# Attention outputs of a graph layer: turned in 32x32 blocks by VectorE and exchanged by DMA, in place of four TensorE transposes

## The chip, the cores and the metric

The kernel runs on one core of a Trainium2 chip. The metric is the device time of one execution in microseconds, lower is better. Engines are named as in the profile: PE is TensorE (PEld its weight loads), DVE is VectorE, ACT is ScalarE, POOL is GpSimd, SP is SyncE, which computes nothing here but issues nearly all DMAs.

## The reference, cut to what matters

There are 16 graphs (B = 16) of N = 1024 nodes with D = 256 features, and a 0/1 adjacency matrix each. Two layers follow each other. The first is multi-head attention with a mask, then an MLP; the second a graph attention that isn't touched here. The part that matters:

```python
normed = layer_norm(x, gamma1, beta1)
qkv = normed.reshape(b_, n_, H, HD).transpose(0, 2, 1, 3)      # H = 8 heads, HD = 32
scores = einsum('bhqd,bhkd->bhqk', qkv, qkv) * scale
attn = softmax(where(adj > 0, scores, -inf))
out = einsum('bhqk,bhkd->bhqd', attn, qkv)
x = x + out.transpose(0, 2, 1, 3).reshape(b_, n_, d_)
y = layer_norm(x, gamma2, beta2)
x = x + gelu(y @ W1 + b1) @ W2 + b2
```

All data are fp32, except the mask, which is held in an 8-bit float.

## The kernel before, in words

`tile_gnn_kernel` calls `fast_path`, and after it a general path that runs only where a flag asks for it; it isn't run on these inputs. `fast_path` is unrolled over all 16 graphs.

**Attention** (`attention`, L966). A graph is done in 32 *units* (`units`, L1048), over two halves of 512 queries (`qh`), in each over two groups of four heads (`g`), in each over eight tiles of 128 keys (`kt`). `scores` (L971) makes the score matmuls (L987) for a unit with keys on partitions and queries along the free dimension, four heads into two PSUM tiles; DVE adds the mask (L1000) and ACT takes the exponential (L1007), whose accumulator gives the softmax denominators `den`, as the mask is symmetric. `weigh` (L1017) multiplies by the values (L1022) into one PSUM tile `o` of 128 x 512, with the 32 features of the four heads on partitions and 512 queries along the free dimension. The pool of `o` has one buffer. Its result has to be turned, since the residual `h` has queries on partitions.

**Turning it** (`finish`, L951). After the eighth tile of keys DVE copies `o` into `os` (L1031). Later PE transposes four 128 x 128 blocks of it into PSUM (`ptos`, L958), DVE multiplies by the reciprocal sums `rl` and writes `ot` (L960), and POOL adds that to `h` (L964). This happens four times a graph, 64 times in all. `invert` (L1038) makes the reciprocals (L1043, L1044), which are complete only in the second half of the queries.

**The rest of a graph** (`rest`, L1100, a generator; call it stream B, and attention stream A). Rows of `h` are taken in four chunks of 256. For a chunk `c`, `prepare` (L1078) measures the norm of `h` on DVE (L739, L740, L742), lets POOL take a power (L744), and normalizes on DVE (L748); `turn` (L1133) transposes on PE (`pty`, L1143), with the scaled result `yT` (L1147); `expand` is the first product (`ph`, L572, evacuated into `hid` by DVE, L1170), and `contract` the second (`po`, L572, added to `xb` by DVE, L1197). `add_residuals` has POOL add bias and residual (L1113, L1114). Then comes the second layer, whose PE work is `lg`, `pa`, `pf`, `pg`, `puT`, and `store` (L1318) with its store L1321. The last outputs of a graph are made by `tails[b]` within the next graph's `rest`.

**What sets the order.** Stream A of graph b + 1 and stream B of graph b are interleaved by a planner at build time (from L1411): each piece has a *place*, and a `clock` that adds up estimated PE time (2.0 per unit of A, the number yielded by each piece of B). `defer(us, f)` emits `f` when that clock has advanced by so much, `turns` holds transposes that PE makes between units, and `make_turns` (L938) emits them. The order thus planned is kept on every engine: the last lines of `fast_path` chain each engine's instructions in the order in which they were emitted. So each engine, SP among them, works through a fixed list and waits at the head of it. `finished` counts the outputs that have been added to `h`; chunks 0 and 1 need those of the first half of the queries (both groups), and chunks 2 and 3 those of the second.

**Masks.** `turn_masks` (L889) fetches adjacency tiles with two DMAs each (L585) into two buffers, converts them on DVE (L592), and a transposing DMA (L902) brings them to the layout that the scores need; `compare_masks` (L909) compares on POOL (L917), with an accumulation on DVE (L924), that the mask is symmetric. All DMAs share eight completion semaphores in turn, and a DMA is issued only when the one eight before it has landed.

Of the kernel before, what the change touches and what calls it, by code (L numbers as in the profile page):

```python
# [9 lines left out]
F32 = mybir.dt.float32  # L10
# [5 lines left out]
ALU = mybir.AluOpType  # L16

P = 128
# [477 lines left out]
def fast_path(  # L496
# [28 lines left out]
    nc = tc.nc  # L525
# [22 lines left out]
    hp = pool("hp", 2)  # L548
    vp = pool("vp", 2)
    midp = pool("midp", 3)  # L550
    ep = pool("ep", 6)
    denp = pool("denp", 2)
    lp1 = pool("lp1", 6)
    tmpp = pool("tmpp", 2)
    smallp = pool("smallp", 3)
# [4 lines left out]
    def ps_tile(shape, name, dtype=F32):  # L560
        return psm.tile(shape, dtype, tag="ps", name=name)
# [386 lines left out]

    finished = {}

    def finish(b, qh, g, rl, ready, os):  # L951
        h = hs[b]
        run_deferred(ready)
        finished[b, qh] = finished.get((b, qh), 0) + 1
        clock[0] += 0.5
        pt = ps_tile([P, TPH, P], f"ptos_{b}_{g}_{qh}")
        for t in range(TPH):
            nc.tensor.transpose(pt[:, t, :], os[:, t * P : (t + 1) * P], ident)  # L958
        ot = tmpp.tile([P, TPH, GH, HD], F32, tag="w2", bufs=5, name=f"ot_{b}_{g}_{qh}")
        nc.vector.tensor_mul(  # L960
            ot, pt.rearrange("p t (j d) -> p t j d", d=HD), rl.unsqueeze(3).to_broadcast([P, TPH, GH, HD])
        )
        ho = h[qh][:, :, g * P : (g + 1) * P]
        nc.gpsimd.tensor_add(ho, ho, ot.rearrange("p t j d -> p t (j d)"))  # L964

    def attention(b, st):  # L966
        va, kT = st["va"], st["kT"]
        den = denp.tile([P, NQH, NT, H], F32, tag="den", name=f"den_{b}")


        def scores(qh, g, kt):  # L971
            qs = slice(qh * QW, (qh + 1) * QW)
            sc = [
                psc.tile([P, 2, QW], F32, tag=f"sc{i}", name=f"s_{b}_{g}_{qh}_{kt}_{i}") for i in range(2)
            ]
# [18 lines left out]
            mb = st[qh][:, kt // 2, :, kt % 2].unsqueeze(1).to_broadcast([P, 2, QW])  # L994
            es = []
            for i in range(2):
                e = ep.tile([P, 2, QW], F32, tag="e", name=f"e_{b}_{g}_{qh}_{kt}_{i}")
                masked = sc[i]
                if 2 * i >= by_pe:
                    nc.vector.tensor_tensor(e, masked, mb, op=ALU.add)  # L1000
                    masked = e
                es.append(e)

                def weights(e=e, masked=masked, i=i):
                    for j in range(2):
                        n = g * GH + 2 * i + j
                        nc.scalar.activation(  # L1007
                            e[:, j], masked[:, j], AF.Exp, scale=SCALE, accum_out=den[:, qh, kt, n : n + 1]
                        )

                if i == 0:
                    weights()
            return es, weights

        acc, os, rl = {}, {}, {}

        def weigh(qh, g, kt, es):  # L1017
            if kt == 0:
                acc[g, qh] = pso.tile([P, QW], F32, tag="o", name=f"o_{b}_{g}_{qh}")
            o = acc[g, qh]  # L1020
            for j in range(GH):
                nc.tensor.matmul(  # L1022
                    o[j * HD : (j + 1) * HD, :],
                    va[:, kt, (g * GH + j) * HD : (g * GH + j + 1) * HD],
                    es[j // 2][:, j % 2, :],
                    start=(kt == 0),
                    stop=(kt == NT - 1),
                )
            if kt == NT - 1:
                c = os[g, qh] = tmpp.tile([P, QW], F32, tag="w2", bufs=5, name=f"os_{b}_{g}_{qh}")  # L1030
                nc.vector.tensor_copy(c, o)  # L1031
                if qh == NQH - 1:
                    close(qh, g)

        def close(qh, g):
            turns.append((1, lambda: finish(b, qh, g, *rl[g, qh], os[g, qh])))

        def invert(qh, g):  # L1038
            r = smallp.tile([P, TPH, GH], F32, tag="rl", name=f"rl_{b}_{g}_{qh}")
            ts, hs_ = slice(qh * TPH, (qh + 1) * TPH), slice(g * GH, (g + 1) * GH)  # L1040

            def f():
                nc.vector.tensor_tensor(r, den[:, 0, ts, hs_], den[:, 1, ts, hs_], op=ALU.add)  # L1043
                nc.vector.reciprocal(r, r)  # L1044

            rl[g, qh] = r, defer(2.5, f)

        units = [(qh, g, kt) for qh in range(NQH) for g in range(NG) for kt in range(NT)]  # L1048
        for u in units:
            make_turns()  # L1050
            es, rest_of_weights = scores(*u)
            go_on()
            rest_of_weights()
            scored.append((weigh, (*u, es)))
            qh, g, kt = u
            if qh == NQH - 1 and kt % TPH == TPH - 1:
                invert(kt // TPH, g)
                if kt < NT - 1:
                    close(kt // TPH, g)
            yield  # L1060

    def go_on():
# [37 lines left out]
    def rest(b, st, tails):  # L1100
# [230 lines left out]
        hid = {0: (yield from expand(0))}  # L1331
        ask(turn, 1)
        yield from tails[b]()
        while finished.get((b, 1), 0) < NG:
            yield 0.0, None
        prepare(b, st, 2)
        load(2)
        hid[1] = yield from expand(1)
        ask(turn, 2)
        prepare(b, st, 3)  # L1340
        yield from contract(0, hid[0])
# [84 lines left out]
    def stream_b():  # L1426
        for b in range(B):
            done = 0.0
            place = b + 0.99
            yield place  # L1430
            for us, others in states[b]["rest"]:
                clock[0] += us
                done += us
                if others is None:

                    if places[1] is None:
                        make_turns()
                    else:
                        place = max(place, places[1] + 1e-6)
                elif others:  # L1440
                    place = max(place, b + 1 + done / B_US)
                yield place
        for us, _ in tails[B]():
            clock[0] += us
            yield B + 1
# [115 lines left out]
```

## Time and profile before

| | |
|---|---|
| Time, median of 3 runs | 3426.13 us (3424.79 to 3426.3) |
| Profiled execution: its own time, its span | 3422.06 us, 3420.3 us |
| Granted TensorE clock | 0.999 |
| `ptos` transposes on PE (L958) | 256, 41.9 us busy |
| Copy `os` from PSUM on DVE (L1031) | 64, 681 ns each |
| Product `ot` on DVE (L960) | 64, 692 ns each |
| Sum into `h` on POOL (L964) | 64, 1284 ns each |
| SP, issue of one store of 128 KB (L1321) | 0.34 us, landed after 1.7 us |
| SP, issue of one mask fetch of 256 KB (L585) | 0.37 us, landed after 3.6 us |
| SP, issue of one transposing DMA (L902) | 1.2 us, landed after 3.9 us |

How to read it: times of single instructions come from one profiled execution; a matmul's end is modelled, so that matmuls that follow each other overlap by a few hundredths of a microsecond in the timeline. The share of an engine is its busy time over the span. A number in brackets behind an instruction is the time that its engine stood idle ahead of it, and what ended that.

### The profile page before, as it was taken

What the parts mean: (1) busy time and instruction counts of PE and PEld (TensorE: products, weight loads), DVE (VectorE), ACT (ScalarE), POOL (GpSimd) and SP (SyncE); (2) the same over time, 40 slices, a digit from 0 to 9 for tenths busy, and PEclk for the clock granted to TensorE, in tenths of its full rate; (3) what the DMA queues carried; (4) which work ended last, traced back from release to release, by engine and by line L of the source; (5) the groups of instructions that cost most, each with busy time, mean ns of one, the idle gap of its engine ahead of it and who ended that gap; (6) DMA issues with size and microseconds to landing.
All of it is one profiled execution on the core that took longest, in us unless ns stands there. A gap on an engine that the chain in (4) does not pass through costs nothing. (4 is left out here: it accounts for less than half of the span.)

```text
span 3420.3 us, 114618 instructions
## 1 busy us (share of the span) xinstructions
PE 3356.2 (98%) x49790; PEld 1603.4 (47%) x49790; DVE 2799.1 (82%) x5427; ACT 2061.6 (60%) x5192; POOL 880.6 (26%) x1038
## 2 busy tenths in 40 slices
PE   6899999999999999999999999999999999999998
PEld 1244444444444444444444444444444444444477
DVE  6788888888888978888888887888879788897854
ACT  6665666656566565666656656666665655666532
POOL 3422232222323222232222312223222232321120
PEclk9999999999999999999999999999999999999999
DMA  4111202112011121111211112120211211111000
GB/s 135 45 39 40 57 17 54 39 47 56 20 46 39 48 54 34 40 31 48 54 39 48 25 50 45 42 56 18 52 39 48 55 26 40 39 48 42 8 19 14
DMA packets 157471, 145.22 MB, mean 42 GB/s; under 512 B 81056, under 2 KB 116256, under 8 KB 156960
## 3 DMA queue, kind: packets, MB, share of 16 engines
q1 hardware_dynamic: 156672, 137.56, 15.8%
q8 instruction: 392, 6.42, 0.8%
q14 instruction: 119, 0.97, 0.1%
q10 hardware_dynamic: 288, 0.26, 0.0%
HBM read 104.21 MB, written 16.78 MB: 35 GB/s over the span
## 5 line engine op out<-in xcount | busy, mean ns | idle before, releaser
L1007 ACT ACTIVATE e<-e 128x512 f32<-128x512 f32 x1984 | 1224.8, 619 | 960.5 <-DVE e L1000 958.1
L1000 DVE TENSOR_TENSOR e<-s,mk 128x1024 f32<-128x1024 f32 x992 | 1168.1, 1218 | 195.2 <-PE s L987 192.7
L987 PE MATMUL s<-kT 32*64 32x512 f32 x8192 | 579.5, 615 | 1.1 <-DVE e L1000 0.9
L1022 PE MATMUL o<-e,va 128*32 128x512 f32 x4096 | 557.5, 606 | 1.3 <-ACT e L1007 1.3
L572 PE MATMUL lg<-fT,uT 128*32 128x256 f32 x7680 | 454.1, 379 | 0.0
L572 PE MATMUL pa<-gw,e 128*32 128x258 f32 x7552 | 453.3, 380 | 0.0
L572 PE MATMUL ph<-yT,w 128*32 128x256 f32 x7808 | 451.0, 379 | 0.0
L572 PE MATMUL po<-w,hid 128*32 128x256 f32 x7680 | 438.9, 379 | 0.0
L1007 ACT ACTIVATION_READ_ACCUMULATOR e<-e 128x1 f32 x1984 | 371.2, 187 | 0.0
L572 PEld LDWEIGHTS ph<-yT,w 128*32 128x32 f32 x7808 | 255.5, 110 | 213.0 <-issue 55.7
L572 PEld LDWEIGHTS lg<-fT,uT 128*32 128x32 f32 x7680 | 257.3, 110 | 200.5 <-issue 43.3
L572 PEld LDWEIGHTS pa<-gw,e 128*32 128x32 f32 x7552 | 252.3, 110 | 206.6 <-issue 56.5
L572 PEld LDWEIGHTS po<-w,hid 128*32 128x32 f32 x7680 | 249.6, 110 | 209.6 <-issue 62.8
L1022 PEld LDWEIGHTS o<-e,va 128*32 128x32 f32 x4096 | 83.6, 108 | 424.6 <-issue 198.9
L1267 DVE SCALAR_TENSOR_TENSOR e<-lg,gw,mk 128x256 f32<-128x256 f32 x512 | 221.7, 474 | 64.2 <-PE lg L572 37.4
L1273 ACT ACTIVATE e<-e,shift 128x512 f32<-128x512 f32 x256 | 182.2, 715 | 141.5 <-DVE e L1272 103.8
L964 POOL TENSOR_TENSOR h<-h,ot 128x512 f32<-128x512 f32 x64 | 84.7, 1323 | 697.8 <-DVE ot L960 697.8
L917 POOL TENSOR_TENSOR odd<-mk,mq 128x512 bf16<-128x512 fp8e5 x192 | 233.3, 1216 | 100.2 <-DVE uneven L924 100.2
L1170 DVE TENSOR_TENSOR hid<-ph,b1c 128x512 f32<-128x512 f32 x256 | 173.6, 683 | 77.8 <-PE ph L572 67.8
L1272 DVE SCALAR_TENSOR_TENSOR e<-e 128x512 f32<-128x512 f32 x256 | 209.5, 818 | 8.8
L987 PEld LDWEIGHTS s<-kT 32*64 32x64 f32 x8192 | 122.7, 130 | 161.0 <-issue 105.0
L744 POOL TENSOR_TENSOR rs_c<-ve_c,mhalf 128x2 f32<-128x2 f32 x64 | 44.5, 695 | 477.4 <-DVE ve_c L742 378.1
(135 smaller groups left out, 3477.0 us busy)
## 6 DMA issues: line engine op xcount, KB each, us to landing
adj<-in_adj_dram SPq DMA_DIRECT2D x248, 256.0 KB, 3.6
h<-in_x_dram SPq DMA_DIRECT2D x64, 256.0 KB, 4.0
xb<-in_x_dram SPq DMA_DIRECT2D x128, 128.0 KB, 2.3
out_dram<-z SPq DMA_DIRECT2D x128, 128.0 KB, 1.7
adj<-in_adj_dram SPq DMA_DIRECT2D x4, 512.0 KB, 7.0
mk<-mq SPq DMA_TRANSPOSE x128, 3.8
w<-in_L_gnn_W_dram SPq DMA_DIRECT2D x2, 1024.0 KB, 8.7
wo<-in_L_gnn_W_dram SPq DMA_DIRECT2D x2, 256.0 KB, 9.8
```

What stands on the lines that cost most here:

```text
L572: nc.tensor.matmul(out[c : c + HD], lhsT[:, c : c + HD], rhs, start=start, stop=stop)
L744: nc.gpsimd.tensor_tensor(rs, ve, mhalf[:, :nt], op=ALU.pow)
L917: nc.gpsimd.tensor_tensor(odd.rearrange("p (u v x) -> p u v x", u=2, v=2), key.rearrange("p (u v x) -> p u v x", u=2, v=2), query.rearrang ...
L964: nc.gpsimd.tensor_add(ho, ho, ot.rearrange("p t j d -> p t (j d)"))
L987: nc.tensor.matmul(sc[j // 2][c : c + P // 2, j % 2, :], kT[r, g, kt * P + c : kt * P + c + P // 2], kT[r, g, qs], start=j >= by_pe, stop= ...
L1000: nc.vector.tensor_tensor(e, masked, mb, op=ALU.add)
L1007: nc.scalar.activation(e[:, j], masked[:, j], AF.Exp, scale=SCALE, accum_out=den[:, qh, kt, n : n + 1])
L1022: nc.tensor.matmul(o[j * HD : (j + 1) * HD, :], va[:, kt, (g * GH + j) * HD : (g * GH + j + 1) * HD], es[j // 2][:, j % 2, :], start=(kt = ...
L1170: nc.vector.tensor_tensor(hid[:, f0 : f0 + 2, :], ph, b1c[:, f0 : f0 + 2].unsqueeze(2).to_broadcast([P, 2, CW]), op=ALU.add,)
L1267: nc.vector.scalar_tensor_tensor(e[:, j, :], lg[:, j, :], gw[:, kt, D : D + 1], st[c // 2][:, kt // 2, qs, kt % 2], op0=ALU.add, op1=ALU.add,)
L1272: nc.vector.scalar_tensor_tensor(e, e, ALPHA, e, op0=ALU.mult, op1=ALU.max)
L1273: ready = defer(2.5, lambda: nc.scalar.activation(e, e, AF.Exp, bias=shift))
```

## The change

DVE's copy of `o` becomes a transpose of 32x32 blocks straight from PSUM into a tile `x`, named `xo` in the profile. Within each block features and queries change places, but the blocks of the four heads are still on four groups of 32 partitions. Sixteen plain DMAs of 16 KB (32 partitions of 512 bytes) then move them, so that each head's block comes to the partitions of its queries: `move(j)` issues four of them, and is deferred by 2, 5, 8 and 11 us of the planner's clock. POOL multiplies by the reciprocal sums and adds to `h`. `finish` and its entry in `turns` are gone; `close` is deferred by 16 us (second half of the queries) or 4.5 us. In `rest`, the check of `finished` and `prepare(b, st, 2)` come after `expand(1)`. The pool `ep` has five buffers for six, the tag `w2` four for five, and a pool `turnp` with one buffer holds `x`. One `clock` addition moves into the planner's loop.

```diff
-    ep = pool("ep", 6)
+    ep = pool("ep", 5)
+    turnp = pool("turnp", 1)
...
-    def finish(b, qh, g, rl, ready, os):
-        h = hs[b]
-        run_deferred(ready)
-        finished[b, qh] = finished.get((b, qh), 0) + 1
-        clock[0] += 0.5
-        pt = ps_tile([P, TPH, P], f"ptos_{b}_{g}_{qh}")
-        for t in range(TPH):
-            nc.tensor.transpose(pt[:, t, :], os[:, t * P : (t + 1) * P], ident)
-        ot = tmpp.tile([P, TPH, GH, HD], F32, tag="w2", bufs=5, name=f"ot_{b}_{g}_{qh}")
-        nc.vector.tensor_mul(
-            ot, pt.rearrange("p t (j d) -> p t j d", d=HD), rl.unsqueeze(3).to_broadcast([P, TPH, GH, HD])
-        )
-        ho = h[qh][:, :, g * P : (g + 1) * P]
-        nc.gpsimd.tensor_add(ho, ho, ot.rearrange("p t j d -> p t (j d)"))
...
             if kt == NT - 1:
-                c = os[g, qh] = tmpp.tile([P, QW], F32, tag="w2", bufs=5, name=f"os_{b}_{g}_{qh}")
-                nc.vector.tensor_copy(c, o)
+                x = turnp.tile([P, GH, TPH, HD], F32, tag="block", name=f"xo_{b}_{g}_{qh}")
+                nc.vector.transpose(x, o.rearrange("p (t a i) -> p a t i", t=TPH, a=GH))
+                c = os[g, qh] = tmpp.tile([P, GH, TPH, HD], F32, tag="w2", bufs=4, name=f"os_{b}_{g}_{qh}")
+
+                def move(j):
+                    for a in range(GH):
+                        nc.sync.dma_start(c[a * HD : (a + 1) * HD, j], x[j * HD : (j + 1) * HD, a])
+
+                for j in range(GH):
+                    defer(2.0 + 3.0 * j, lambda j=j: move(j))
                 if qh == NQH - 1:
-                    close(qh, g)
-
-        def close(qh, g):
-            turns.append((1, lambda: finish(b, qh, g, *rl[g, qh], os[g, qh])))
+                    close(qh, g, 16.0)
+
+        def close(qh, g, us):
+            def f():
+                finished[b, qh] = finished.get((b, qh), 0) + 1
+                c = os[g, qh].rearrange("p j t d -> p t j d")
+                ho = hs[b][qh][:, :, g * P : (g + 1) * P].rearrange("p t (j d) -> p t j d", d=HD)
+                nc.gpsimd.tensor_mul(c, c, rl[g, qh].unsqueeze(3).to_broadcast([P, TPH, GH, HD]))
+                nc.gpsimd.tensor_add(ho, ho, c)
+
+            defer(us, f)
...
-                    close(kt // TPH, g)
+                    close(kt // TPH, g, 4.5)
...
         yield from tails[b]()
+        hid[1] = yield from expand(1)
         while finished.get((b, 1), 0) < NG:
             yield 0.0, None
         prepare(b, st, 2)
         load(2)
-        hid[1] = yield from expand(1)
         ask(turn, 2)
...
                         make_turns()
+                        clock[0] += 0.5
```

More of the change, by code (lines that the diff above doesn't have):

```diff
@@ L1029, in weigh @@
             if kt == NT - 1:
-                c = os[g, qh] = tmpp.tile([P, QW], F32, tag="w2", bufs=5, name=f"os_{b}_{g}_{qh}")
-                nc.vector.tensor_copy(c, o)
-                if qh == NQH - 1:
-                    close(qh, g)
-        def close(qh, g):
-            turns.append((1, lambda: finish(b, qh, g, *rl[g, qh], os[g, qh])))
+                x = turnp.tile([P, GH, TPH, HD], F32, tag="block", name=f"xo_{b}_{g}_{qh}")
[6 more added lines that the diff above has]
+                    defer(2.0 + 3.0 * j, lambda j=j: move(j))
+                if qh == NQH - 1:
+                    close(qh, g, 16.0)
[7 more added lines that the diff above has]
+            defer(us, f)
         def invert(qh, g):
-            r = smallp.tile([P, TPH, GH], F32, tag="rl", name=f"rl_{b}_{g}_{qh}")
-            ts, hs_ = slice(qh * TPH, (qh + 1) * TPH), slice(g * GH, (g + 1) * GH)
+            r = rl[g, qh] = smallp.tile([P, TPH, GH], F32, tag="rl", name=f"rl_{b}_{g}_{qh}")
+            ts, heads = slice(qh * TPH, (qh + 1) * TPH), slice(g * GH, (g + 1) * GH)
             def f():
-                nc.vector.tensor_tensor(r, den[:, 0, ts, hs_], den[:, 1, ts, hs_], op=ALU.add)
+                nc.vector.tensor_tensor(r, den[:, 0, ts, heads], den[:, 1, ts, heads], op=ALU.add)
                 nc.vector.reciprocal(r, r)
-            rl[g, qh] = r, defer(2.5, f)
+            defer(2.5, f)
         units = [(qh, g, kt) for qh in range(NQH) for g in range(NG) for kt in range(NT)]
```

## The prediction, made before the result was known

> **What bounds the kernel now.** I read first the busy shares, then the same by stage, then the operations that the change removes, then the timeline around the places it touches.
>
> ```profile
> PE 3356.2 (98%) x49790; PEld 1603.4 (47%) x49790; DVE 2799.1 (82%) x5427; ACT 2061.6 (60%) x5192; POOL 880.6 (26%) x1038
> ...
> 1470.00:1680.00 210.00, 209.04 (x3228) 97.99 (x3224) 177.61 (x342) 129.06 (x325) 55.06 (x65) 1.00 0.17 45
> ```
>
> The second line is one stage of 210 us, about one graph (columns: the stage, then busy time of PE, PEld, DVE, ACT, POOL, then clock and DMA). PE is busy for 209.0 of 210 us and every stage but the first and last looks alike; DVE has 32 us to spare, ACT 81, POOL 155. So PE's own instructions and PE's waits set the end, and work moved to DVE, POOL or DMA is free as long as PE never waits for it.
>
> ```profile
> L958 PEld LDWEIGHTS ptos<-ident,os x256: 137/141/143, 91.8 to 3269.6; 128*128 128x128 f32 x128
> L958 PE MATMUL ptos<-ident,os x256: 272/273/329, 91.8 to 3269.8; 128*128 128x128 f32 x128
> L960 DVE TENSOR_TENSOR ot<-ptos,rl x64: 679/692/693, 97.3 to 3270.1; 128x512 f32<-128x512 f32 x64
> ...
> L1031 DVE COPY os<-o x64: 679/681/682, 52.9 to 3268.6; 128x512 f32<-128x512 f32 x64
> ```
>
> These are the operations at stake (ns, shortest/median/longest). The change also shifts a norm (`prepare(b, st, 2)`); here is its neighbourhood in one graph:
>
> ```profile
> 1634.29 1.91 PE L572 MATMUL ph<-yT,w 128*32 128x256 f32 x32
> ...
> 1636.01 3.64 PE L572 MATMUL po<-w,hid 128*32 128x256 f32 x64
> ...
> 1636.87 0.41 DVE L924 TENSOR_TENSOR uneven<-uneven,odd 128x256 int32<-128x256 int32 x1
> ...
> 1637.20 0.42 DVE L739 BATCH_NORM_STATS2 st_c<-h 128x6 f32<-128x256 f32 x1
> ...
> 1638.40 0.17 DVE L742 TENSOR_SCALAR ve_c<-mv_c 128x2 f32<-128x2 f32 x1
> ...
> 1638.65 0.69 POOL L744 TENSOR_TENSOR rs_c<-ve_c,mhalf 128x2 f32<-128x2 f32 x1 [8.96 <-DVE ve_c L742]
> ...
> 1639.58 0.66 PE L1143 MATMUL pty<-ident,y 128*128 128x128 f32 x4
> 1639.72 0.42 DVE L1197 TENSOR_TENSOR xb<-po,xb 128x256 f32<-128x256 f32 x1 [1.14 <-PE po L572]
> ```
>
> The columns are start, length, engine, line. The norm is that of chunk 3; chunk 2's was done some 10 us before, so that the four `pty` transposes (chunk 2) follow `po` without a gap.
>
> **What the Trainium skill says.** "VectorE: DVE Perf Modes", section "The three transpose paths", says that VectorE turns 32x32 blocks only, and gives 311 ns for 128x128 bf16, less than TensorE's 390. The nearest row here is the copy of the same 128x512 fp32 out of PSUM, 681 ns. I go by that row. "DMA: Bandwidth & Descriptors", section "Rules for kernel authors", says that transfers under 64 KB pay mostly overhead. The moves are 16 KB. This trace has no such size: stores of 128 KB land in 1.7 us, loads of 128 KB in 2.3, of 256 KB in 3.6. I take 2 us per move, and what matters is whether anybody waits.
>
> **The change, part by part.** I compared the order of instructions of both programs: PE's is the same but for the `ptos` transposes, ACT's is the same entirely. So each effect is a PE interval that goes or a PE wait that comes.
>
> *Transposes removed.* In PE's timeline I measured at all 64 places the time from the end of the matmuls before to the start of the score matmuls behind, less the hand-over of -0.07 us that this pair has elsewhere. A place without a wait costs 0.59 us. In graphs 1 to 14 the four places cost 1.05 (0.38 of it a wait for ACT L1249), 0.59, 0.59 and on average 1.12 us (the last waits for the copy of `os`): 3.35 us a graph, 47.0 in all. The last graph has 2.6. The first has 4.9, but at its first two places DVE or ACT would hold PE anyway, so I count 4 x 0.6 = 2.4. Gone: **52 us**. (The 256 matmuls' busy time alone is 41.9.)
>
> *Copy becomes block transpose, product leaves DVE.* 64 copies of 681 ns become 64 transposes. Not below 0.68, since each still passes 512 columns from PSUM; above, twice that, 1.36, if fp32 goes at half rate. I take 0.7. The 64 products L960 (44 us of DVE) leave, so even at 1.36 DVE's sum is unchanged. After each copy DVE's mask add ends about 3.4 us before PE's next score matmul needs it (1611.5 against 1614.96 at one place), so 0.68 more is hidden. The single buffer `xo` is wanted again after 8 units, some 51 us. Cost 0; up to 5 us at the upper end, if the shorter PE period uses up the slack.
>
> *Moves on SP.* 16 per unit of eight, 1,024 in all. SP's nearest issue rows are 0.34 us (store L1321) and 0.37 (L585) below, 1.2 (the transposing DMA L902) above. I take 0.37: 24 us of a graph's 207 on SP. Nothing in the program holds a burst back to its planned time; SP issues as waits permit: the block transpose, the moved tile free, and the eighth DMA before having landed. So 16 moves take 6 to 8 us, and the last lands about 10 us after the transpose. In front of them SP only waits for things as old; behind them stand mask fetches L585, transposing DMAs L902, loads of `h` and `xb`, stores. The tightest is the fetch after a unit's end: now issued at 1658.02, landed near 1662.4, converted by DVE L592 at 1663.85. With four moves of 0.37 in front from 1657.1, the fetch ends issuing at 1659.4 and lands near 1663.0. Still in time, 0.85 us spare.
>
> *Product and sum on POOL.* Another 1.28 us (row L964, same size) per place, 82 us, in 155 us a graph of idle POOL. The tightest reader is chunk 0's norm: reciprocal done at 1577.9, two POOL operations to 1580.6, norm at 1585.4. While POOL reads SBUF it can hold up VectorE operations with two SBUF inputs; bounded by 82 us times a small share, hidden in DVE's spare time. The product waits for all 16 moves, and behind it on POOL stand `h`/`xb` sums and the mask comparisons L917, for which DVE's L924 waits. In the tightest graph part the moves land near 1617, the sums and the comparison are through by 1621.5, and L924 wants it at 1630. Cost 0.
>
> *Buffers, clock.* The sixth `ep` buffer isn't needed: by PE's order the old reader precedes the score matmuls that lead to the new writer. `w2` holds only four live tiles. PE's unchanged order shows that the clock edits cancel.
>
> *The norm that moves.* `expand(1)` now stands ahead of the check for finished sums, and `prepare(2)` behind it. Yet `pty` of chunk 2 keeps its place on PE. DVE now does both norms between L924 and L1197: chunk 2's 1637.20 to 1638.57, chunk 3's (another 1.37) to 1639.94, then L1197 (0.35 until the next can start) to 1640.3, then the two normalizations (0.73) to 1641.05. The second transpose needs the second of them; it started at 1639.72 and would start at 1641.1. **PE stands 1.4 us** in each of 15 graphs: 21 us. Bounds 0.7 (if DVE arrives earlier, relieved of L960) and 2.2 (POOL's power late). DVE's following work slips by as much as PE's, so no second wait. In the last graph the expansion of chunk 1 ends at 3289.8; evacuation 3290.6, norm 3292.0, power 3292.75, normalization 3293.6, `pty` at 3293.65 instead of 3290.2: 3.4 us. Given back: **24 us**.
>
> *Sum.* -52 + 21 + 3.4 = -27.6. The profiled execution took 3422.06 (span 3420.3): 3394.5. The runs' median lies 4.1 above it: **3398 us**.
>
> **Rivals.** (1) *The stall does not appear* because DVE is enough ahead: the full 52, or 45 with a stall of 0.5 us: 3374 to 3381. For it: DVE loses 0.69 us per place. Against: DVE's start there is set by PE (the evacuation of `ph`), not by DVE's backlog. (2) *Part of the rest is lost too*, to a slow block transpose, port contention or the shorter slack: another 10 to 25 us, 3408 to 3423. (3) *Slower: the mask fetches behind the moves.* If a move holds SP for m us instead of 0.37, the fetch above is late by 1657.1 + 4m + 0.8 (its issue) + 3.6 - 1663.85 = 4m - 2.35 us. The next one stands behind twelve more moves, a load (0.4) and a transposing DMA (1.2), and is late by 16m - 11.3 against its conversion at 1675.2; the unit that ends at 1554.0 gives 16m - 10.7 in the same way. At m = 1.0 these are 1.7, 4.7 and 5.3; beyond some 3 us of slack (the 3.4 above) PE loses 1.7 + 2.3 = 4 us a graph, 60 in 15: 3458. It cancels the gain (27.6 / 15 = 1.85 us a graph) from about m = 0.93, between the issue rows of 0.37 and 1.2. Against: a move is the plain kind, whose rows say 0.34 to 0.46. That the bursts don't pace anything is part of this.
>
> **How the numbers follow.** Forecast (3388 to 3408) 0.50; rival 1 0.20; rival 2 0.15; rival 3 0.15. The range 3374 to 3422 leaves out rival 3 and small tails. Within 0.2% (3419 to 3433), about what a measurement of this kernel can tell from no change, lies a third of rival 2: 0.05. Faster 0.80, slower 0.15.
>
> **What would show it.** PE's busy time falls by about 42 us. A wait of `pty` for DVE `y` near 1.4 us, 15 times, appears, absent now. `xo` has a row near 0.7 us. SP's moves have a median near 0.37; DVE L592 waits for `adj` no more than now (3.8 us in 4 waits). A block transpose over 3 us, moves over 0.7 us on SP, or DVE waiting for POOL's L924 input would make the prediction wrong.

## The result, and the profile after

The changed kernel takes **3477.88 us** (median of 4 runs, 3474.48 to 3481.10), against 3425.68 for the kernel before on the same chip. The ratio is 1.0152, with a 95% interval of 1.0135 to 1.0170, so it is slower by 52 us. The forecast was 3398. The profiled execution took 3481.1 us (span 3479.3), 59.0 more than that of before.

The busy shares, from the page of the changed kernel:

```profile
PE 3379.2 (97%) x49534; PEld 1620.0 (47%) x49534; DVE 2812.3 (81%) x5363; ACT 2061.9 (59%) x5192; POOL 955.1 (27%) x1102
```

The 256 transposes are gone (49534 matmuls for 49790), and with them 41.9 us of work, yet PE's busy time is 23 us longer. Busy time grows when the two halves of a row of matmuls run one after the other instead of together, or when they run at a lower clock. DVE's busy time is 13 us longer than before, although 64 products (44 us) have left it. The same stage of 210 us as in the prediction, and one of 30 us in the first graph (columns as there: the stage, busy PE, PEld, DVE, ACT, POOL, then clock, DMA share, GB/s):

```profile
120.00:150.00 30.00, 23.16 (x216) 4.59 (x211) 13.55 (x28) 16.77 (x52) 3.02 (x3) 0.83 0.38 97
1470.00:1680.00 210.00, 207.01 (x3172) 97.56 (x3160) 174.31 (x329) 125.86 (x323) 57.36 (x66) 1.00 0.18 47
```

In the steady stage PE stands 3 us where it stood 1. In the first graph it does much worse, and its clock is 0.83 where it was 1.00. The waits of PE on VectorE (columns: total us, times, longest):

```profile
PE pty L1143 <- DVE y L749: 24.7, 18, 4.9
PE s L972 <- DVE e L985: 24.0, 25, 2.6
```

The first wait is the one that the prediction named; before it was 1.6 us in 2. The second is new (0.9 before). The operations of the change, by tile:

```profile
L1021 SPq DMA_DIRECT2D os<-xo x1024: 507/589/2087, 54.1 to 3335.1; - x171
L1016 DVE STREAM_TRANSPOSE xo<-o x64: 703/706/717, 53.4 to 3324.0; 128x512 f32<-128x512 f32 x64
L1033 POOL TENSOR_TENSOR os<-os,rl x64: 1043/1048/1087, 111.4 to 3337.2; 128x512 f32<-128x512 f32 x64
```

The block transpose costs what was forecast. A move holds SP 0.59 us in the median and up to 2.1, not 0.37. And VectorE's waits for the mask, before and after:

```profile
DVE mq L592 <- DMA adj<-in_adj_dram: 3.8, 4, 1.7
DVE mq L593 <- DMA adj<-in_adj_dram: 49.4, 54, 4.8
```

**Where PE falls behind.** PE's order is the same in both programs but for the transposes, so each PE row of one trace can be set beside its partner in the other. I call the difference of their start times the lag. It is 20.5 us at the end of the first graph (220 us of the old trace), grows to 57.1 in the next fourteen, 2.6 a graph, and ends at 59.0. In the graph of the prediction's timeline it moves like this: -1.04, -0.59, -0.59 and -0.88 us at the four places of the transposes, as measured in the prediction (3.1 in sum), but +1.9 right behind the first, +3.3 ahead of chunk 0's transposes, +0.9 behind the last, and +1.06 at chunk 2's. Only the last of these was in my sum.

The +3.3 starts on SP (columns: start, length, operation, count), after the unit that ends at 1593:

```profile
1594.75 3.91 SPq L1021 DMA_DIRECT2D os<-xo  x4
1598.77 1.00 SPq L586 DMA_DIRECT2D adj<-in_adj_dram  x2
1599.82 8.78 SPq L1021 DMA_DIRECT2D os<-xo  x12
1608.64 1.27 SPq L903 DMA_TRANSPOSE mk<-mq  x1
1610.01 0.99 SPq L586 DMA_DIRECT2D adj<-in_adj_dram  x2
```

Four moves take 3.9 us and the other twelve 8.8. Fourteen of the sixteen hold SP for 0.51 to 0.72 us, and two for 2.1 and 1.8; the DMAs eight before these two had landed by then, and what held them stays open. The second pair of fetches starts at 1610.0. In the old trace it started at 1565.2, which at this place's lag would be about 1603. VectorE and PE, some rows later:

```profile
1614.90 0.43 DVE L593 TENSOR_SCALAR mq<-adj 128x512 fp8e5<-128x512 int32 x1 [3.63 <-DMA adj<-in_adj_dram]
...
1621.29 2.21 PE L972 MATMUL s<-kT 32*64 32x512 f32 x16 [0.93 <-DVE e L985]
```

VectorE stands 3.6 us for the mask, and its next mask add is late by so much that PE stands 0.9 us before the score matmuls and about as long inside them (2.21 us for a row that takes 1.11). This is rival 3.

The +1.9 behind the first place has nothing to do with the moves:

```profile
1568.23 1.17 POOL L918 TENSOR_TENSOR odd<-mk,mq 128x512 bf16<-128x512 fp8e5 x1
...
1568.26 1.17 DVE L743 TENSOR_SCALAR ve_b<-mv_b 128x2 f32<-128x2 f32 x1
...
1573.06 2.22 PE L972 MATMUL s<-kT 32*64 32x512 f32 x16 [0.88 <-DVE e L985]
```

An addition of two numbers per partition, 0.17 us before, took 1.17: it ended when GpSimd's comparison did. The same three rows in the old trace:

```profile
1528.71 1.61 POOL L917 TENSOR_TENSOR odd<-mk,mq 128x512 bf16<-128x512 fp8e5 x1
...
1530.42 0.17 DVE L742 TENSOR_SCALAR ve_b<-mv_b 128x2 f32<-128x2 f32 x1
...
1535.16 1.29 PE L987 MATMUL s<-kT 32*64 32x512 f32 x16
```

There the comparison was over (1530.32) before the addition began; the new product has pushed it back. VectorE has no gap from 1559.85 to here, so that the microsecond reaches PE. With it comes the gain of the transposes handed back (1.04), as turns_out will show. VectorE is rid of the product here (about 0.6), but another of its rows, beside GpSimd too, takes 1.33 us for 0.88 (at 1565.81); together that is the 1.9.

**The clock.** The trace also records the clock that PE was granted. In the old kernel it is halved once for 3.4 us, and again in the last microseconds; the changed one has those last ones too, and before them four halvings in the first graph (20 us together) and five of 3.4 us in later ones. Four of these five follow the stall just shown: at 513.68 the score matmuls come 0.89 us late, with the second half 1.1 us behind the first, and from 515.6 to 519.0 the clock is half. The fifth follows the last graph's norm. Each of the five adds about 1.5 us to the lag, 7.7 in all, and those of the first graph some 6, so that some 13 of the 59 us come by way of the clock.

### The profile page after: what moved, and what is told of

Read it like the earlier page. It is cut to its first block, busy times and chain, and to the rows that moved or that the text cites. A ratio compares the mean times of both kernels' runs of the same rounds, so it can differ in the third digit from the quotient of the medians.

```text
span 3479.3 us, 115406 instructions
## 1 busy us (share of the span) xinstructions
PE 3379.2 (97%) x49534; PEld 1620.0 (47%) x49534; DVE 2812.3 (81%) x5363; ACT 2061.9 (59%) x5192; POOL 955.1 (27%) x1102
## 3 DMA queue, kind: packets, MB, share of 16 engines
q14 instruction: 129, 1.06, 0.1%
## 5 line engine op out<-in xcount | busy, mean ns | idle before, releaser
L972 PE MATMUL s<-kT 32*64 32x512 f32 x8192 | 614.1, 617 | 25.1 <-DVE e L985 24.0
L1007 PE MATMUL o<-e,va 128*32 128x512 f32 x4096 | 575.6, 610 | 1.3 <-ACT e L992 1.3
L573 PE MATMUL pa<-gw,e 128*32 128x258 f32 x7552 | 465.2, 380 | 0.9 <-DVE e L1267 0.9
L573 PE MATMUL lg<-fT,uT 128*32 128x256 f32 x7680 | 462.4, 381 | 0.0
L573 PEld LDWEIGHTS lg<-fT,uT 128*32 128x32 f32 x7680 | 265.5, 111 | 199.5 <-issue 57.3
L573 PEld LDWEIGHTS pa<-gw,e 128*32 128x32 f32 x7552 | 265.8, 110 | 196.8 <-issue 43.4
L1033 POOL TENSOR_TENSOR os<-os,rl 128x512 f32<-128x512 f32 x64 | 67.1, 1048 | 788.1 <-DMA os<-xo 346.6
L918 POOL TENSOR_TENSOR odd<-mk,mq 128x512 bf16<-128x512 fp8e5 x192 | 225.5, 1179 | 95.5 <-DVE uneven L925 90.6
L815 POOL TENSOR_TENSOR nrm<-nrm,g 128x256 f32<-128x256 f32 x128 | 101.5, 793 | 207.5 <-DVE nrm L749 207.5
```

Source lines behind the costliest of these rows:

```text
L573: nc.tensor.matmul(out[c : c + HD], lhsT[:, c : c + HD], rhs, start=start, stop=stop)
L815: nc.gpsimd.tensor_mul(nrm, nrm, g1)
L918: nc.gpsimd.tensor_tensor(odd.rearrange("p (u v x) -> p u v x", u=2, v=2), key.rearrange("p (u v x) -> p u v x", u=2, v=2), query.rearrang ...
L972: nc.tensor.matmul(sc[j // 2][c : c + P // 2, j % 2, :], kT[r, g, kt * P + c : kt * P + c + P // 2], kT[r, g, qs], start=j >= by_pe, stop= ...
L1007: nc.tensor.matmul(o[j * HD : (j + 1) * HD, :], va[:, kt, (g * GH + j) * HD : (g * GH + j + 1) * HD], es[j // 2][:, j % 2, :], start=(kt = ...
L1033: nc.gpsimd.tensor_mul(c, c, rl[g, qh].unsqueeze(3).to_broadcast([P, TPH, GH, HD]))
```

## The experiments

Unless said otherwise a difference is between medians, against the kernel before, run beside it on the same chip.

**One part alone, in the kernel before.**

```diff
 (moves_only: sixteen moves after each copy, into a tile that nobody reads)
                 nc.vector.tensor_copy(c, o)
+                y = turnp.tile([P, GH, TPH * HD], F32, tag="block", name=f"dummy_{b}_{g}_{qh}")
+                xs = c.rearrange("p (a f) -> p a f", a=GH)
+                def move(j):
+                    for a in range(GH):
+                        nc.sync.dma_start(y[a * HD : (a + 1) * HD, j], xs[j * HD : (j + 1) * HD, a])
+                for j in range(GH):
+                    defer(2.0 + 3.0 * j, lambda j=j: move(j))
```

> The kernel before with nothing of the change but its sixteen moves: after each copy of a unit the same sixteen 16 KB moves are issued by SP at the same places, from the copied tile into a tile that nobody reads (and one buffer of the weights fewer, to make room). The output is as before. Theory Q (the moves hold SP, so that mask fetches and loads land late, DVE waits for them in order and PE for DVE): the trace of the changed kernel has lost 20 us against the old one by 220 us of its span, and up to 1.6 us twice in each later graph; so 3426 + 20 + 15 x 1.5 = about 3468, with DVE waiting for the mask some 50 us where it waited 3.8. Rival C (the loss comes from VectorE and GpSimd getting in each other's way, or from the norm): the moves alone cost nothing, 3426.

Measured 3449.89 against 3423.39: **+26.5 us** (1.0078, 1.0063 to 1.0094). VectorE's waits for the mask:

```profile
DVE mq L593 <- DMA adj<-in_adj_dram: 37.1, 50, 4.5
```

The moves cost time with the rest of the change absent (but for one `ep` buffer fewer) and nobody reading what they move. VectorE's waits, for the mask and for `h` (22.1 us, 3.1 before), point at SP's order; masks_ahead below tests that. The cost is 16 us short of what I read out of the changed kernel. The lag tells where: 13.3 in the first graph, then 15 in the next fourteen, 1.1 a graph, where I had put 1.5.

```diff
 (norm_only)
+        hid[1] = yield from expand(1)
         while finished.get((b, 1), 0) < NG:
             yield 0.0, None
         prepare(b, st, 2)
         load(2)
-        hid[1] = yield from expand(1)
```

> The kernel before with only the expansion of chunk 1 put ahead of the norm of chunk 2. Theory N (my step on the norm, with the size that the changed kernel's trace shows): the transposes of chunk 2 wait for VectorE 1.06 us in 15 graphs and some 3 us in the last: 3426 + 16 + 3 = 3445. By the prediction's own size, 1.4 us and 3.4: 3450. Rival (the stall was a product of the other parts, VectorE having fallen behind): no change, 3426.

Measured 3447.28: **+23.9 us** (1.0071, 1.0057 to 1.0084).

```profile
PE pty L1143 <- DVE y L748: 20.3, 17, 3.4
```

Theory N holds. The single wait is 1.06 us; the first graph costs 3.7 and the last one 5 instead of 3. In the last one PE stands 3.38 us, as forecast, and then the clock is half for 3.4 us, which adds 1.6; the first graph's 3.7 are made of 2.1 and such a 1.6 too.

```diff
 (pool_only)
+        nc.gpsimd.tensor_mul(ot, ot, ones4.unsqueeze(3).to_broadcast([P, TPH, GH, HD]))
         nc.gpsimd.tensor_add(ho, ho, ot.rearrange("p t j d -> p t (j d)"))
```

> The kernel before with only a second GpSimd operation in each place, a product of the same size (by ones, so that the output is as before). Theory C (GpSimd's longer work falls on VectorE operations that it holds up): in the changed kernel's trace a 0.17 us operation took 1.17 us behind the mask comparison, and another 1.33 instead of 0.88, once in most graphs. Here the old transposes still stand there, and VectorE still has the product L960, so 0.5 to 1.5 us in 15 graphs: 3433 to 3448. Rival (the collisions fall into VectorE's spare time): 3426.

Measured 3434.59: **+11.2 us** (1.0036, 1.0022 to 1.0050). The lag grows by 0.8 in most graphs, at the place of the comparison shown above (0.79 behind the score matmuls of 1535.16). Fourteen of the additions `ve_b` take about 1.2 us here, none before. Theory C holds at the lower end of its size.

```diff
 (turns_out)
-        for t in range(TPH):
-            nc.tensor.transpose(pt[:, t, :], os[:, t * P : (t + 1) * P], ident)
+        pt = os.rearrange("p (t q) -> p t q", t=TPH)
...
-                nc.vector.reciprocal(r, r)
+                nc.vector.tensor_scalar_mul(r, r, 1e-30)
```

> The kernel before without its 256 transposes: VectorE's product reads the copied sums themselves (rows stand in the wrong partitions), and the reciprocal is replaced by a product with 1e-30 of the same size, which leaves the attention's sum out of the result. Copy, product and sum stay on their engines, SP and the norm are untouched. The prediction's step (a place without its transposes gains what PE spends there, 3.35 us a graph): 3423 - 52 = 3371. Rival B (at these places VectorE is the next to hold PE, so that most of it is given back within two units): what the three runs with one part each leave for it is 52 - 26.5 - 23.9 - 11.2 = -9 us, 3414; by the no-moves trace (3.1 us gained a graph, of which some 0.9 and 0.8 are given back to VectorE), about 1.4 x 15 = 21, 3402.

Measured 3404.23 against 3422.72: **-18.5 us** (0.9942, 0.9928 to 0.9955), where the prediction's step said -52. This is the run that hits the forecast hardest. The lag shows the gain at all four places (-1.04, -0.59, -0.59, -0.88) and its return: +1.7 within three units of the first, +0.71 after the last; the other two keep theirs. The rows behind the first place in this kernel:

```profile
1521.81 0.63 PE L822 MATMUL ptk<-ident,va 128*128 128x128 f32 x4 [0.46 <-DVE e L1265]
...
1528.18 2.22 PE L985 MATMUL s<-kT 32*64 32x512 f32 x16
```

```profile
1515.14 0.88 DVE L1265 SCALAR_TENSOR_TENSOR e<-lg,gw,mk 128x256 f32<-128x256 f32 x2 [1.38 <-ACT e L1005]
...
1521.43 1.27 POOL L962 TENSOR_TENSOR h<-h,ot 128x512 f32<-128x512 f32 x1
...
1521.70 1.55 DVE L1270 SCALAR_TENSOR_TENSOR e<-e 128x512 f32<-128x512 f32 x1
...
1526.91 2.34 DVE L998 TENSOR_TENSOR e<-s,mk 128x1024 f32<-128x1024 f32 x2
```

Behind the `e` row of 1515.14, up to 1530, no VectorE row names a wait. PE arrives 1 us earlier, waits 0.46 us for VectorE at 1521.81, and then 1.1 us inside the score matmuls at 1528.18 (2.22 us for 1.11) until the mask add of 1526.91 has freed the second half. Rival B's larger figure, 21 us, is near. The old trace had the sign of it: the same row took 1.29 us there, so VectorE already set that meeting.

The stand-in is not quite clean, however. Its product reads two tiles of SBUF, where the old one read one of them from PSUM, and VectorE's row of 1521.70 takes 1.55 us beside GpSimd's sum where it took 0.88. That is 0.67 of the 1.7 us given back, and without it the return equals the gain (1.04). Over the trace this kind of row is 9.6 us longer than before, so the transposes alone may be worth up to some 28 us (an estimate: 18.5 and these 9.6), still half of 52.

```diff
 (turns_out_pool, on top of turns_out)
-        nc.vector.tensor_mul(
+        nc.gpsimd.tensor_mul(
             ot, pt.rearrange("p t (j d) -> p t j d", d=HD), rl.unsqueeze(3).to_broadcast([P, TPH, GH, HD])
```

> The kernel before without its 256 transposes, as in turns_out (rows in the wrong partitions, the attention's sum left out by the product with 1e-30), and with the product on GpSimd; no moves, the norm in its old place. It is the remaining pair of the change's parts. If the parts add: 3404 + 11 = 3415. If a VectorE relieved of 0.69 us at each place lets the gain of the transposes through: 3385 to 3395. If the four parts make up the whole: 3478 - 26.5 - 24 = 3427.

Measured 3410.03 against 3423.40: **-13.4 us** (0.9958, 0.9944 to 0.9972). Moving the product costs nothing clearly outside the intervals here (5 us more than turns_out), and brings nothing in sum. At the first place 1.86 us are given back for 1.04 gained, as in the changed kernel; after the last place 0.33 instead of 0.71. But the clock differs: in this kernel's trace it is halved seven times in the later graphs, each time behind the first place (here the score row with its wait, and the next row, which usually takes 1.07 us), and each time the lag grows by about 1.6 us; in turns_out's later graphs it never is.

```profile
490.03 2.22 PE L985 MATMUL s<-kT 32*64 32x512 f32 x16 [0.87 <-DVE e L998]
492.17 2.42 PE L1020 MATMUL o<-e,va 128*32 128x512 f32 x8
```

So what VectorE is relieved of goes to GpSimd and to the clock, and this run cannot say how much to each.

**One part undone, in the changed kernel.**

```diff
 (no_moves: turnp with four buffers, c is x, no DMAs)
-                c = os[g, qh] = tmpp.tile([P, GH, TPH, HD], F32, tag="w2", bufs=4, name=f"os_{b}_{g}_{qh}")
+                os[g, qh] = x
...
-                nc.vector.reciprocal(r, r)
+                nc.vector.tensor_scalar_mul(r, r, 1e-30)
```

> The changed kernel without its moves: GpSimd's product reads the turned tile itself (four buffers of it in place of the moved tile's four), so rows stand in the wrong partitions; and the reciprocal is replaced by a product with 1e-30 of the same size on VectorE, which leaves the attention's sum out of the result. Theory Q: the 43 us that the fetches behind the moves cost come back, 3478 - 43 = 3435; what stays is the norm's 19 us and what VectorE and GpSimd do to each other. If Q is wrong and VectorE against GpSimd is the cause: 3470 to 3478. If all but the norm is due to the moves: 3398, my forecast.

Measured 3450.62 against 3423.39: +27.2 us (1.0070, 1.0054 to 1.0087), so 25 less than the changed kernel: the moves again, from the other side. The 25 is rough: one of the four runs took 3438.18 us, at a granted clock of 0.997, the other three 3450 to 3452, at 0.992 or 0.993. VectorE waits 5.5 us for the mask. The first graph is still 11.2 us behind, of which the norm explains 3.7. The rest is seen in PE's rows there:

```profile
135.28 1.06 PE L1007 MATMUL o<-e,va 128*32 128x512 f32 x8
141.14 0.47 PE L1137 MATMUL pty<-ident,y 128*128 128x128 f32 x1 [4.79 <-DVE y L749]
142.48 0.90 PE L1137 MATMUL pty<-ident,y 128*128 128x128 f32 x3 [0.87 <-DVE y L749]
143.32 1.04 PE L573 MATMUL s<-mk,ident 128*32 128x512 fp8e5 x8
144.29 2.01 PE L972 MATMUL s<-kT 32*64 32x512 f32 x16
```

The sums of the early half, closed with a delay of 4.5 us, now come right ahead of the norm that reads them; VectorE waits 2.5 us for GpSimd's sum, its four normalizations take 3.76 us beside GpSimd's next product (2.27 in a later graph of norm_only), and PE stands 4.8 us. Then the matmuls run at half speed (2.01 us for 1.11). In the old kernel this stall was 1.35 us.

```diff
 (norm_back)
-        hid[1] = yield from expand(1)
         while finished.get((b, 1), 0) < NG:
             yield 0.0, None
         prepare(b, st, 2)
         load(2)
+        hid[1] = yield from expand(1)
```

> The changed kernel with the expansion of chunk 1 put back behind the norm of chunk 2 (two statements exchanged, nothing else). PE's order is the same. Theory N, that the parts add: 3476 - 24 = 3452. Rival: the norm now waits for the sixteen moves and for GpSimd, whose sum is late, so VectorE stands in order behind it: 3470 or more.

Measured 3459.26 against 3422.72: +36.5 (1.0104, 1.0088 to 1.0119), 16 less than the changed kernel. The larger part of the 24 comes back; VectorE's wait for the mask stays (49.5 us).

```diff
 (masks_ahead: adjp with four buffers, one tile more in flight)
-        raw = fetch_mask(b, ts[0])
+        raws = [fetch_mask(b, ts[0]), fetch_mask(b, ts[1])]
...
-            if i + 2 < TPH:
-                raw = fetch_mask(b, ts[i + 2])
+            if i + 3 < TPH:
+                raws.append(fetch_mask(b, ts[i + 3]))
```

> The changed kernel with the mask tiles fetched two ahead instead of one (four buffers of halves instead of two); the moves stay on SP as they are. The output is as before. Theory Q, in its narrow form (the moves cost what VectorE waits for masks that land late): the 49 us of waits for the mask shrink to under 10, and most of the 27 us that the moves cost comes back, 3476 - 20 = 3456; the loads of h and xb stand behind the moves as before. If the moves cost by something else (their own landing, the late sums, the on-chip memory): no change, 3470 to 3478.

Measured 3454.36 against 3422.45: +31.9 (1.0093, 1.0078 to 1.0109), **20 less** than the changed kernel with all 1,024 moves still on SP. VectorE's list of waits no longer has the mask (for `h` it still waits 25.8 us). So most of what the moves cost is the fetch behind them that lands late: the narrow form of theory Q. Fetching ahead in the old kernel was not run; it waits only 3.8 us for the mask, so there could be little to gain there.

```diff
 (moves_on_act)
-                        nc.sync.dma_start(c[a * HD : (a + 1) * HD, j], x[j * HD : (j + 1) * HD, a])
+                        nc.scalar.dma_start(c[a * HD : (a + 1) * HD, j], x[j * HD : (j + 1) * HD, a])
```

> The changed kernel with its 1,024 moves issued by ScalarE's queue instead of SP's; nothing else. Theory Q: SP's fetches are on time again, minus 27 us; but ScalarE is held for some 0.6 us a move, 9.6 us a unit of 52, of its 21 idle: the exponentials come late where four moves fall between them, 2.4 us at a time, some of which PE waits for. I expect 3455 to 3475. If SP's order is not the cause: above 3478, since ScalarE's time comes on top.

Measured 3544.21 against 3422.45: +121.8 (1.0349, 1.0333 to 1.0365). My size was far off. A move holds ScalarE as long as SP (0.60 us), and ScalarE also stands 128 us waiting for earlier moves ahead of exponentials; by the lag PE loses some 7 us a graph. This run does not tell the theories apart.

```diff
 (product_on_dve)
-                nc.gpsimd.tensor_mul(c, c, rl[g, qh].unsqueeze(3).to_broadcast([P, TPH, GH, HD]))
+                nc.vector.tensor_mul(c, c, rl[g, qh].unsqueeze(3).to_broadcast([P, TPH, GH, HD]))
```

> The changed kernel with the product back on VectorE (from the moved tile), the sum staying on GpSimd; nothing else. If GpSimd's longer work costs here what it cost alone (11 us) and VectorE's 0.69 us per place costs nothing: 3476 - 11 = 3465. If VectorE is what PE meets next at these places: 0.69 in three places of 15 graphs comes on top, 31 us at most, so 3465 to 3490. My prediction's step (the product's move costs nothing and brings nothing): 3476.

Measured 3489.39 against 3422.45: +66.9 (1.0191, 1.0175 to 1.0206), 15 more than the changed kernel. The size lies in the second case, but for a reason that I had not written down:

```profile
DVE os L1033 <- DMA os<-xo: 48.6, 30, 6.3
```

VectorE, in order, now waits for the moves itself. By the lag 10 of the 15 us are lost in the first graph, where the clock is half for 37 us instead of 20.

```diff
 (five_dmas: x written to memory, read back by four)
+                s = dramp.tile([GH, P, TPH, HD], F32, tag="s", name=f"scr_{b}_{g}_{qh}")
+                defer(2.0, lambda: nc.sync.dma_start(s.rearrange("a p t d -> p a t d"), x))
+                def back():
+                    for a in range(GH):
+                        nc.sync.dma_start(c[a * HD : (a + 1) * HD], s[a].rearrange("(j i) t d -> i j t d", i=HD))
+                defer(5.0, back)
```

> The changed kernel with the exchange of partitions in five DMAs in place of sixteen: one writes the turned tile to memory, four read it back in the new order. The output is as before. Theory Q: SP is held by 5 issues instead of 16 (4 us where it was 11), so nearly all of the 27 us that the moves cost comes back: 3476 - 22 = about 3454. If what costs is the bytes on the DMA rings or the writes into the on-chip memory, and not SP's order, it stays at 3470 or more, since the bytes double.

Measured 3464.84 against 3422.72: +42.1 (1.0123, 1.0108 to 1.0139), 10 less than the changed kernel. VectorE's waits for the mask fall to 8.1 us, yet less than half of the moves' cost comes back. By the lag the first graph ends 12.7 behind (20.5 with the moves), and later graphs still lose 1.9 each. Between that and 3454 I have no cause.

**Mended versions.**

```diff
 (mended: five_dmas, norm_back, and)
-                    close(qh, g, 16.0)
+                    close(qh, g, 9.0)
...
-                nc.gpsimd.tensor_mul(c, c, rl[g, qh].unsqueeze(3).to_broadcast([P, TPH, GH, HD]))
+                nc.vector.tensor_mul(c, c, rl[g, qh].unsqueeze(3).to_broadcast([P, TPH, GH, HD]))
 (mended_2, on top of mended: masks_ahead, and in graph 0 the old copy, transposes and product)
 (mended_3, on top of mended_2: close 12.5 us after the unit, and the early products at the old kernel's place)
+            elif us < 5.0:
+                turns.append((0, lambda: (run_deferred(rl_due[g, qh]), f())))
```

> The change with its three costs taken away: five DMAs through memory in place of sixteen moves, the norm of chunk 2 ahead of the expansion, the sums closed 9 us after the unit in place of 16, and the product on VectorE, as before the change. The block transpose stays and the transposes of TensorE stay away. The output is as before. If the parts add: what the transposes alone bring (9 to 52 us) less some 5 us for the five DMAs: 3380 to 3420, faster than both kernels. If the DMAs or the later sums cost as much as the moves did: 3430 to 3440.

Measured 3442.13 against 3422.72: +19.4 (1.0056, 1.0042 to 1.0070). Slower still. Half of it is the first graph (10.6 us of lag); VectorE waits 48.9 us for the moved tile and 9.1 for the mask.

> The mended kernel with two edits more: masks fetched two ahead, and the first graph, in which PE is not the bound, left with the old way (copy, transposes of TensorE, product from there). The output is as before. By the traces: the mended kernel stood 10.6 us behind the old one when the first graph was over, and lost about 1 us in each later graph, at the two conversions behind the five DMAs. Without both: the gain that the transposes alone gave, about 1.1 us in 15 graphs: 3442 - 10.6 - 15 to 20 = 3411 to 3416, faster than both kernels by 0.2 to 0.3%. If the later loss isn't the masks': 3431.

Measured 3436.67 against 3422.45: +14.2 (1.0042, 1.0029 to 1.0056). The first graph is level (lag 0.5), but a later one loses 1.1 where turns_out gains 1.2:

```profile
DVE os L1055 <- DMA os<-scr: 52.6, 30, 3.3
```

> The mended kernel of the last call with the products put where the old kernel has them in VectorE's order (ahead of the next unit's mask add; a unit's last product 12.5 us after its end instead of 9, so that the five DMAs have landed). The output is as before. If what mended_2 lost in its later graphs (1.07 us behind the conversions, and 0.8 us more than turns_out at the last place) comes from these two places of the product: 3437 - 15 x 1.9 = 3408, close to turns_out's 3404. If it comes from the DMAs themselves: 3430 to 3437.

Measured 3414.70 against 3423.40: **-8.7 us** (0.9976, 0.9966 to 0.9987). VectorE's list has neither `os` nor `adj`, though it now waits 20.5 us for stores to land. Of the versions that do the whole computation it alone beats the old kernel, by a sixth of what was forecast for the transposes; its first graph still has them. The expectation of 3408 was 7 us too good.

## Why the prediction was wrong

| step | forecast | alone | what it was |
|---|---|---|---|
| transposes removed | -52 | -18.5 | gain at all places, two thirds given back, to VectorE first |
| block transpose | 0 | not run alone | 0.706 us a row (0.7 taken) |
| moves on SP | 0 | +26.5 | 0.59 us to issue, masks late |
| product on GpSimd | 0 | +11.2 | its longer work holds up VectorE |
| norm | +24.4 | +23.9 | 1.06 us a graph, more at both ends by the clock |
| granted clock | no term | not run alone | half for 38 us, 3 in the old kernel (the end left out) |
| sum | -27.6 | +43 | whole change +52 |

**Transposes removed.** The step measured at each place what PE spends on the transposes, and took that for the gain: "52 us". The intervals were right to a tenth. What failed is that a PE interval that goes is a gain only as far as the next engine that PE meets is ahead by as much. I asked for VectorE's reserve at one place (3.4 us, at 1611 to 1615) and in the sum of a stage (32 us), and not at the first place, where it is nil. Turns_out shows it: -18.5 us, or at most some 28 if the stand-in's own loss is added back.

**Moves on SP.** "I take 0.37", and of the tightest fetch "Still in time, 0.85 us spare". The issue is 0.59 us in the median, and 0.98 and 0.73 on average in the two bursts shown. I had worked out rival 3 and the point at which it decides (0.93), and gave it 0.15 because a move is "the plain kind". The nearest row for that (128 partitions from memory) was no bound for 32 partitions from one on-chip tile to another. The mechanism is rival 3's. Its size in the later graphs (forecast 60 at 1.0 us) is 15 alone. What I left out altogether is the first graph, where the copies follow each other every 30 us (at 53, 82, 114 and 144) and not every 52: 13 of the 26.5 us by the lag. Moves_only shows both, and masks_ahead that the late masks carry most of it.

**Product and sum on POOL.** I bounded what GpSimd does to VectorE by "82 us times a small share, hidden in DVE's spare time". There is no spare time at the place where it falls. "GPSIMD Engine Reference" of the Trainium skill, section "Specifications", says that GpSimd shares its SBUF interfaces with VectorE, and names two kinds of VectorE instruction that contend. That agrees with the row above, 1.17 us for 0.17 beside a comparison of 1.17; which of the two kinds this addition is, no run here shows. The step named VectorE operations with two SBUF inputs; such a one is the row of 1521.70 in turns_out, 1.55 us for 0.88 beside GpSimd's sum, but this addition reads only one tile. That the product also delays the comparison that collides was not in the step.

**The norm that moves.** Right in mechanism and, alone, in size (24.4 forecast, 23.9 measured). That the size agrees is in part luck: the single wait is 1.06 instead of 1.4 us, and two halvings of the clock, of which the step knew nothing, made up 3.2 us. Rival 1, that the stall does not appear, fails.

**Buffers, clock.** The edits to the planner's clock left PE's order alone, as said. But `close` 4.5 us after its unit is a change of the planner too. I traced its reader in a later graph only ("norm at 1585.4"), and in the first one it makes VectorE wait 2.5 us for a sum.

**The granted clock.** The sum has no term for it. That PE stands for a microsecond was taken to cost a microsecond, but some of these stalls were followed by a half clock, and then the same stall cost 1.5 us more. No run takes this apart from its causes; the 13 us above are read from the lag.

**What stays open.** Moves (+26.5), norm (+23.9), and transposes with the product on GpSimd (-13.4) add to +37, and the whole is +52. Intervals of some 5 us each do not cover 15. One part of the difference is seen: the late sums of the first graph, which no_moves has and the three runs don't (11.2 us of lag against 3.7 and 0.7). For the rest, the lag says that the moves cost 22 us in the later graphs of the changed kernel and 15 alone. That fits a VectorE whose reserve the other parts have used, but this is argued, not shown. The clock blurs all these sums, as no_moves shows with 12 us between runs of one program.

## What to carry to other kernels

Before counting a removed PE interval as a gain, look at PE's next two or three rows on the same tiles: a row that is longer than its kind (1.29 us for 1.11 here) can mean that another engine already sets that meeting, and that the gain ends there. Price a DMA's issue by a row of its own shape, and if there is none, follow what is queued behind it at the upper bound, in the densest stage of the program and not only in the steady one. When work goes to an engine with idle time, check what that engine shares with the one that is short of it. Compare the granted clock of two kernels before giving the whole difference to waits.

## What the runs showed of the hardware

**The clock falls after a short stall.** In the changed kernel's first graph:

```profile
129.97 1.09 PE L972 MATMUL s<-kT 32*64 32x512 f32 x8
133.65 1.98 PE L972 MATMUL s<-kT 32*64 32x512 f32 x8 [2.60 <-DVE e L985]
135.56 1.94 PE L1007 MATMUL o<-e,va 128*32 128x512 f32 x8
...
138.28 2.01 PE L972 MATMUL s<-kT 32*64 32x512 f32 x16
140.22 1.06 PE L1007 MATMUL o<-e,va 128*32 128x512 f32 x8
```

A wait of 2.6 us is followed by 6.6 us of matmuls at about half speed, which cost another 3.1 us (the rows less their usual 1.09, 1.06, 0.61 and 1.11). So a stall there costs twice. In later graphs a wait of 0.9 us with a score row of 2.2 behind it was enough: four times in the changed kernel, seven in turns_out_pool, though not in every graph. Away from the end, a halving lasts 3.4 us or a multiple of it in all these traces, and the starts in one trace lie whole multiples of 3.413 us apart. That would explain why only some of these stalls are followed by one, but no run tests it. Over the first 210 us the granted clock is 0.94, 0.99, 0.83 and 0.89 in the four stages of 30 us from 60 to 180; in the old kernel only the last of them is below 1.00 (0.94). "TensorE: Matmul & The Clock Gate" of the Trainium skill, section "HAM oscillation", warns of idle gaps above about 3.4 us; these were shorter, and the measurement decides.

**A small DMA is not cheaper to issue.** A 16 KB move between on-chip tiles holds SP 0.507 us at the least, and ScalarE 0.513. In mended_3 the write of 256 KB to memory takes 0.377 and a read of 64 KB back 0.424 (medians); these land in 2.3 and 2.9 us, the moves in 1.8.
